# A two-layer network with routed experts: weighting at the eviction, adding gathers, and a regrouped schedule

## The chip, the core and the metric

The kernel runs on one core of a Trainium2 chip. The core has a matrix engine (TensorE, PE in the profile, with PEld for its weight loads), a vector engine (VectorE, DVE), an activation engine (ScalarE, ACT), a general engine (GpSimd, POOL) and an engine that issues most transfers (SyncE, SP). Each works through its own list of instructions in order, and semaphores tie them together. Matrix products land in PSUM, which has eight banks of 128 rows by 512 floats; tiles live in SBUF, 128 partitions wide; tensors of the program and its scratch live in device memory. The metric is the device time of one execution in microseconds (us), less is better. Everything is in 32-bit floats, except the one-hot matrices of the routing, which are in 16 bits. A 32-bit product is issued as two matmul passes, so the profile counts two matmuls for each.

## What is computed

The input has 4 sequences of 1024 tokens with 256 features. Two layers follow each other; each has a sequence part and a feed-forward part, and after each part the input is added and the row normalised:

```python
x = layernorm(x + ssd(x))            # state-space scan, 2 heads of 128, state 64
x = layernorm(x + gelu_mlp(x))       # 256 -> 1024 -> 256
x = layernorm(x + linear_attn(x))    # 16 heads of 16, 64 exponential features, causal
x = layernorm(x + experts(x))        # below

def experts(xf):
    shared = sum(ffn(xf, sw1[i], sw2[i], sw3[i]) for i in range(2))
    rw, sel = top_k(xf @ router_w.T + expert_bias, 2)      # of 8 experts
    rw = softmax(rw)
    combine = einsum("tk,tke->te", rw, one_hot(sel, 8))
    return shared + sum(combine[:, e, None] * ffn(xf, w1[e], w2[e], w3[e]) for e in range(8))

def ffn(x, w1, w2, w3):
    return silu(x @ w1.T) * (x @ w3.T) @ w2.T              # 256 -> 512 -> 256
```

The linear attention keeps, for each head, a running sum of products of key features and values, and a running sum of the key features. An output is the query's features times that sum, divided by the query's features times the sum of keys.

## The kernel before

**Blocks and stream.** The 4096 tokens are 8 blocks of 512, each of 4 tiles of 128 tokens. The stream of a block, `xs[i]`, stays in SBUF from beginning to end and every part adds to it in place.

**Order of the work, first section.** PE's order up to the routed experts is laid out before the program is built: each piece of work is a `Task` with an estimated cost, a rank, the tasks that it comes after with a wait for each, the number of PSUM banks that it takes from one of two pools (6 and 2 banks), and how long it holds them. `trace_tasks` (L239) takes again and again the task that can start first. Only PE is bound to that order; the order of DVE, ACT, POOL and SP is the tool's own, from the dependences and the order in which the program was written. Scan, feed-forward, attention and the first blocks of the shared experts are interleaved in this way.

**Attention.** For a tile of 128 tokens, `scores` makes the masked products of key and query features within the tile, `turn_keys` and `advance` the new contribution to the running sums (`state`), `turn_state` (L667) turns `state` into the stationary tile `kv`, and `outputs` (L627) sums, for each head, the part from the tile itself (`own`, the product with `sc`) and the part from all earlier tiles (the product with `kv`). In `kv` every head has 128 rows, of which 64 hold its state and the others are zero. Four heads fill the four 32-column strips of one bank `ps_o`, and ACT copies the bank to `oraw`.

**Routing.** When the attention of a block is done, `attn_tail` stores its stream turned (`td`) and plain (`xt`) to device memory and `router` (L762) finds the two experts of each token with their weights `wgt`. After the last block `dispatch` (L799) counts the tokens of each expert, gives each token two places (`slot`) in a list that is sorted by expert and padded to 71 tiles, and builds two one-hot matrices for each place: `in_lane` (which row of a tile) and `in_tile` (which tile, times the token's number). `invert` (L882) multiplies them with 64 matmuls into `sent`: which token stands in each row of each tile. All of `dispatch` is traced at one point, in `open_routed`.

**Shared experts.** `shared_jobs` (L890) gives a list of jobs: per block eight hidden jobs (four weight passes for two banks, silu on ACT, the product `gT` on DVE) and four output jobs. Blocks 0 to 4 are run in the first section. Their sums are copied by ACT, stored to device memory (`sd`), and fetched and added again by POOL during the routed stage (`add_part`, L1182). Blocks 5 to 7 are run after the routed experts, and DVE adds their sums straight to the stream (L934).

**Routed experts.** `slot_tiles` (L951) goes over the 71 tiles. `turn` gathers 128 rows of `xt` with an indirect DMA issued by POOL and transposes them, `hidden` multiplies with the weights of the tile's expert (read from a register), `turn_hidden` transposes the result, and `output` multiplies with the second weights, copies (ACT) and stores to `yg`. The gathered tile has six buffers.

**Order of the work, last section.** From the end of the routed stage PE, DVE and ACT run in the order in which the program is written (L1195). After each of the remaining shared jobs one tile is combined (`combine_tile`, L1022): two gathers from `yg`, one for each expert of a token, and two DVE operations that multiply with the weight and add to the stream. When a block lacks nothing, `last_norm` (L1035) computes its statistics and scales on DVE at once, and ACT and SP finish it one job later.

Of the kernel before, what the change touches and what calls it, by code (L numbers as in the profile page):

```python
# [74 lines left out]
def two_layers(ctx: ExitStack, tc: tile.TileContext, x, xT, vecs, cols, wx, w1, w2, wqkv, wout, om, rw, moe, out):  # L75
# [78 lines left out]
    sd = dram.tile([NBLK, P, NT, D], F32, name="sd")  # L154
    xt = dram.tile([NTOK, D], F32, name="xt")
# [4 lines left out]
    wgt = const.tile([P, 2, NTOK // P], F32, name="wgt")  # L160
# [3 lines left out]
    sent = const.tile([P, NSLOT], I32, name="sent")  # L164
    whose = const.tile([1, NSLOT], mybir.dt.int32, name="whose")
# [97 lines left out]
    ssd_end, ffn_end, proj_end, tail_end = {}, {}, {}, {}  # L263
# [208 lines left out]

    def attn_front(hb, wk):
# [109 lines left out]
    def attn_back(hb, wk):  # L583
# [43 lines left out]
        def outputs(j):  # L627

            qf, v1 = front[hb][0], front[hb]["v"]
            tok = slice(j * P, (j + 1) * P)  # L630
            first = hb % 4 == 0 and j == 0
            ps_o = bank(f"ps_o{hb}_{j}", 0)
            for g in range(4):
                for own in ((True,) if first else (False, True)):
                    for c in range(4):
                        h = 4 * g + c
                        f, s = h // 2, h % 2
                        nc.tensor.matmul(  # L638
                            ps_o[c * VW : (c + 1) * VW, g * P : (g + 1) * P],
                            v1[:, j, h, :] if own else kv[:, h, :],  # L640
                            sc[j][f // 4][:, 4 * s + f % 4, :] if own else qf[:, f % 4, f // 4, tok],
                            start=first or not own,
                            stop=own,
                        )
            o[j] = wk.att.tile([P, 4 * P], F32, tag="oraw", name=f"oraw{hb}_{j}", bufs=2)
            nc.scalar.copy(o[j], ps_o)

        def advance(j):
# [3 lines left out]
            for q in range(2):  # L652
                for s in range(2):
                    for r in range(4):
                        nc.tensor.matmul(
                            ps_v[r * VW : (r + 1) * VW, (2 * q + s) * NF : (2 * q + s + 1) * NF],
                            v1[:, j, 8 * q + 2 * r + s, :],
# [9 lines left out]
        def turn_state(j):  # L667
# [4 lines left out]
            for s in range(2):  # L672
                rows = slice(s * NF, (s + 1) * NF)
                nc.scalar.copy(
                    kv[rows].rearrange("p (f s) e -> p f s e", s=2)[:, :, s, :],
                    ps_kv[rows, : 2 * P].rearrange("p (f e) -> p f e", e=VW),
                )
# [517 lines left out]
    with tc.manual_schedule(  # L1195
# [25 lines left out]
        while left:  # L1221
            left.pop(0)()
# [72 lines left out]
```

## Time and profile before

| | before |
|---|---|
| median of 3 runs | 1610.33 us (1609.95 to 1613.02) |
| the profiled execution: its time | 1613.2 us |
| its span, first to last instruction | 1611.5 us |
| PE busy, matmuls | 1518.4 us, 9744 |
| DVE, ACT, POOL busy | 762.5, 605.9, 507.5 us |
| granted PE clock, mean | 0.978 of full |
| gathers of the routed stage, `xe` | 71, 0.944 us of POOL each |
| gathers of the last section, `y` | 64, 0.946 us of POOL each |
| part additions on POOL | 5, 2.35 us each |
| copies of shared sums on ACT, `so` | 10, 0.585 us each |

A line of a timeline gives the start, the length, the engine, the line of the kernel, the operation, output and input tiles, and how many instructions are merged in it; brackets hold the idle time just before it and the instruction that ended it. A line of the list of waits gives who waited, for whom, and then the total, the number of times and the longest. PE's matmuls are pipelined, so the length of one is not the distance between two.

### The profile page before, as it was taken

Reading aid. Unit: us, or ns where it says so; the run is one execution under the profiler, and the core shown is the slowest. Engines: PE = TensorE matmul, PEld = TensorE weight load, DVE = VectorE, ACT = ScalarE, POOL = GpSimd, SP = SyncE. Lnnn points to the kernel's source line nnn. Section 1 sums busy time; section 2 is a strip of 40 time slices with the busy share of each in tenths; the row PEclk is TensorE's granted clock in tenths of the full one; section 3 lists DMA queues with packets and bytes.
Section 4 is the critical chain, followed back from the end, with each engine's and each line's share of the span. In section 5 each row is a group of like instructions: output and inputs, shape, how many; then the busy total and the mean of one; then the engine's idle time right before and its main releaser. Section 6 shows DMA issues by size and latency. Waiting matters only on the chain.

```text
span 1611.5 us, 25591 instructions
## 1 busy us (share of the span) xinstructions
PE 1518.4 (94%) x9744; PEld 998.9 (62%) x9744; DVE 762.5 (47%) x2290; ACT 605.9 (38%) x1065; POOL 507.5 (31%) x524
## 2 busy tenths in 40 slices
PE   8999978999899989899999998999999999999987
PEld 5575656667576757666767665556666666665554
DVE  6977724754646555565544453122222222223765
ACT  2555364454545563554546421122222222221221
POOL 5623323442344332523332215051111111103541
PEclk9999999999999999999999999999999999999999
DMA  8000000000000000200101062331111111111432
GB/s 316 1 1 1 1 1 1 27 1 1 27 2 27 1 14 15 92 27 14 40 1 47 8 231 93 107 112 46 45 44 46 44 46 46 46 33 57 128 101 69
DMA packets 42359, 79.09 MB, mean 49 GB/s; under 512 B 5152, under 2 KB 30880, under 8 KB 40704
## 3 DMA queue, kind: packets, MB, share of 16 engines
q1 hardware_dynamic: 33312, 53.47, 9.3%
q0 software_dynamic: 7200, 20.33, 4.5%
q10 hardware_dynamic: 1728, 3.67, 0.6%
q8 instruction: 80, 1.31, 0.4%
q14 instruction: 39, 0.32, 0.1%
HBM read 52.93 MB, written 24.51 MB: 48 GB/s over the span
## 4 chain that ended last, share of the span: by engine, by line
PE 73%; DVE 14%; ACT 9%; POOL 2%; issue 2%; DMA 0%; SPq 0%; DVEq 0%; ACTq 0%; POOLq 0%
PE ps_ge L975 15%; PE ps_g L908 11%; PE ps_ye L997 8%; PE ps_e L926 6%; PE ps_f L444 5%; PE ps_h L432 5%; PE ps_sc L602 3%; PE ps_o L638 3%; PE ps_gT L990 2%; PE ps_qk L488 2%; PE ps_bc L279 2%; PE ps_k L624 1%; PE ps_p L550 1%; PE ps_v L513 1%; ACT L435 1%
## 5 line engine op out<-in xcount | busy, mean ns | idle before, releaser
L975 PE MATMUL ps_ge<-w,xeT 128*128 x568 | 257.4, 596 | 2.3 <-ACT xeT L968 2.1
L908 PE MATMUL ps_g<-xTs,w 128*128 128x512 f32 x512 | 230.4, 603 | 12.9 <-DVE gT L917 6.8
L958 POOL DMA_INDIRECT xe<-xt,sent x71 | 67.6, 952 | 350.4 <-PE ps_xe L966 329.7
L908 PEld LDWEIGHTS ps_g<-xTs,w 128*128 128x128 f32 x512 | 96.7, 193 | 127.3 <-issue 107.8
L975 PEld LDWEIGHTS ps_ge<-w,xeT 128*128 128x128 f32 x568 | 102.9, 191 | 105.7 <-issue 103.4
L985 DVE TENSOR_TENSOR ge<-se,ps_ge 128x512 f32<-128x512 f32 x71 | 48.8, 687 | 219.1 <-PE ps_ge L975 219.1
L432 PE MATMUL ps_h<-xT,w_sb 128*128 128x512 f32 x256 | 127.8, 643 | 22.3 <-ACT hT L435 12.9
L997 PE MATMUL ps_ye<-w2e,geT 128*128 x568 | 134.4, 379 | 0.0
L926 PE MATMUL ps_e<-w,gT 128*128 128x256 f32 x512 | 120.4, 392 | 10.5 <-DVE x L934 10.5
L444 PE MATMUL ps_f<-w_sb,hT 128*128 128x256 f32 x512 | 118.1, 385 | 1.6 <-ACT hT L435 1.6
L926 PEld LDWEIGHTS ps_e<-w,gT 128*128 128x128 f32 x512 | 99.0, 196 | 30.9 <-DVE x L934 12.9
L997 PEld LDWEIGHTS ps_ye<-w2e,geT 128*128 128x128 f32 x568 | 102.5, 190 | 12.3 <-ACT ye L1005 0.8
L444 PEld LDWEIGHTS ps_f<-w_sb,hT 128*128 128x128 f32 x512 | 96.6, 192 | 17.4 <-issue 3.1
L992 DVE COPY geT<-ps_gT 128x512 f32<-128x512 f32 x71 | 49.1, 692 | 114.4 <-PE ps_gT L990 114.4
L917 DVE TENSOR_TENSOR gT<-sl,ps_g 128x512 f32<-128x512 f32 x64 | 43.9, 686 | 118.0 <-PE ps_g L908 81.8
L432 PEld LDWEIGHTS ps_h<-xT,w_sb 128*128 128x128 f32 x256 | 49.4, 203 | 80.0 <-issue 54.1
L1026 POOL DMA_INDIRECT y<-yg,slot x64 | 63.1, 986 | 99.9 <-PE ps_g L908 47.8
L614 DVE TENSOR_TENSOR sc<-ps_sc,mask_le 128x512 f32<-128x512 f32 x96 | 62.6, 684 | 62.2 <-PE ps_sc L602 53.1
L983 ACT ACTIVATE se<-ps_ge 128x512 f32<-128x512 f32 x71 | 42.4, 597 | 125.5 <-PE ps_ge L975 125.5
L563 POOL TENSOR_SCALAR qf<-qf,csq 128x512 f32<-128x512 f32 x32 | 50.2, 1570 | 116.4 <-ACT qf L561 115.1
L916 ACT ACTIVATE sl<-ps_g 128x512 f32<-128x512 f32 x64 | 37.7, 594 | 130.4 <-PE ps_g L908 100.9
L612 POOL TENSOR_TENSOR sc<-sc,mask_le 128x512 f32<-128x512 f32 x32 | 41.1, 1283 | 133.2 <-ACT sc L611 133.1
(244 smaller groups left out, 2645.6 us busy)
## 6 DMA issues: line engine op xcount, KB each, us to landing
yg<-ye SPq DMA_DIRECT2D x71, 128.0 KB
w<-in_moe SPq DMA_DIRECT2D x8, 1024.0 KB
xt<-in_xT SPq DMA_DIRECT2D x8, 512.0 KB
x<-in_x SPq DMA_DIRECT2D x8, 512.0 KB
xt<-x SPq DMA_DIRECT2D x8, 512.0 KB
td<-xTr SPq DMA_DIRECT2D x16, 256.0 KB
w2e<-in_moe SPq DMA_DIRECT2D x8, 512.0 KB
out<-x SPq DMA_DIRECT2D x7, 512.0 KB
```

Source lines behind the costliest of these rows:

```text
L432: nc.tensor.matmul(ps, w1_sb[:, k, m * P : (m + 1) * P], v.xT[:, k, :], start=(k == 0), stop=(k == KC - 1))
L444: nc.tensor.matmul(v.ps[:, j % 2, :], v.hT[:, m, j * P : (j + 1) * P], w2_sb[:, m, :], start=(m == 0), stop=(m == HID0 // P - 1),)
L563: nc.gpsimd.tensor_scalar_mul(f, f, csq)
L614: nc.vector.tensor_mul(t_s, ps_s, mask)
L908: nc.tensor.matmul(ps[s], w[e][:, 2 * s + k, m * P : (m + 1) * P], xT[i][:, k, :], start=(k == 0), stop=(k == KC - 1),)
L926: nc.tensor.matmul(ps, gT[i, e][:, m, j * P : (j + 1) * P], w2e[:, m, :], start=(e == 0 and m == 0), stop=(e == NSH - 1 and m == HID // P ...
L958: nc.gpsimd.indirect_dma_start(out=xe, out_offset=None, in_=xt, in_offset=bass.IndirectOffsetOnAxis(ap=sent[:, s : s + 1], axis=0),)
L975: nc.tensor.matmul(pg[a], xeT[s][:, k, :], w13[:, bass.ds(e * (4 * HID) + (2 * a + k) * HID, HID)], start=(k == 0), stop=(k == KC - 1),)
L985: nc.vector.tensor_mul(ge[s], se, pg[1])
L992: nc.vector.tensor_copy(geT[s].rearrange("p m t -> p (m t)"), ps)
L997: nc.tensor.matmul(ps[:, :D], geT[s][:, m, :], w2[:, bass.ds(of[s] * (2 * HID) + m * D, D)], start=(m == 0), stop=(m == HID // P - 1),)
L1026: nc.gpsimd.indirect_dma_start(out=y, out_offset=None, in_=yg, in_offset=bass.IndirectOffsetOnAxis(ap=slot[:, n, t : t + 1], axis=0),)
```

## The change

There are six edits.

- **64-row states.** `kv` has one 64-row half for each head, and two heads share a column of it. In `outputs` the product with the past takes 64 rows, from the half that `half_of` gives; heads whose numbers differ by four lie in opposite halves of the array and in different banks, so `ps_o` becomes two banks, with two groups of heads each. The order is: past of two groups, own part of the two, and the same for the other two groups. ACT copies two banks of half a width; `turn_state` copies once. The estimates of the task are changed (1.6 instead of 2.0, two banks, held 1.4).
- **One-hot steps.** `dispatch` returns its eight pairs of comparisons and the list of experts as steps; each is a task of its own among the shared jobs. The token numbers are counted so that the sign of `token_no` says nothing of the place, and the two places of a token are summed in two PSUM areas, which gives `nth`: whether a row of a tile is its token's first or second choice.
- **Direct sums.** The shared sums of blocks 0 to 4 are added by DVE to the stream, two tiles at a time; the copies, stores, loads and additions by POOL are gone. A shared job now comes after the store of its block (`turn_end`).
- **Weights on eviction.** The rows of `xt` have two more columns with the token's two weights, stored by `router`. A gathered tile brings them along; two small DVE operations pick the right one (`xew`), and ACT scales the routed output with it when it evicts it.
- **First tile ahead.** The gather, the transposes and the copy of the first routed tile are a task before the last shared job of the first section.
- **Adding gathers and norms in parts.** `combine` fetches a block's rows with gathers that add into the stream in the DMA itself (`compute_op`), the first choices of four tiles and then the second ones. Five blocks are issued after the second job of the last section, the others after their turn. `last_norm` is cut into sums, scales and finish, each placed behind a job of its own.

```diff
-    xt = dram.tile([NTOK, D], F32, name="xt")
+    xt = dram.tile([NTOK, D + 2], F32, name="xt")
+    xtv = xt.rearrange("(t p) d -> p t d", p=P)
...
+    def half_of(h):
+        return (h ^ h >> 2) & 1
...
-            ps_o = bank(f"ps_o{hb}_{j}", 0)
-            for g in range(4):
+            ps_o = [bank(f"ps_o{hb}_{j}_{n}", 0) for n in range(2)]
+            o[j] = wk.att.tile([P, 4 * P], F32, tag="oraw", name=f"oraw{hb}_{j}", bufs=2)
+            for gs in ((0, 1), (2, 3)):
                 for own in ((True,) if first else (False, True)):
...
+                    for g in gs:
+                        for c in range(4):
+                            h = 4 * g + c
+                            f, s = h // 2, half_of(h)
+                            rows = slice(s * NF, (s + 1) * NF)
+                            nc.tensor.matmul(
+                                ps_o[g % 2][c * VW : (c + 1) * VW, g // 2 * P : (g // 2 + 1) * P],
+                                v1[:, j, h, :] if own else kv[rows, f, :],
+                                sc[j][f // 4][:, 4 * s + f % 4, :] if own else qf[rows, f % 4, f // 4, tok],
...
+            for n in range(2):
+                nc.scalar.copy(
+                    o[j].rearrange("p (g n t) -> p n g t", n=2, t=P)[:, n],
+                    ps_o[n][:, : 2 * P].rearrange("p (g t) -> p g t", t=P),
+                )
...
+            nc.scalar.copy(kv.rearrange("p f e -> p (f e)"), ps_kv[:, : 2 * P])
...
-                lambda j=j: outputs(j), 2.0, r + 0.02, [(t_c, 4.0), (before.get("kv"), 2.5), (far.get("to"), 0.0)], 0, 1, 1.2
+                lambda j=j: outputs(j), 1.6, r + 0.02, [(t_c, 4.0), (before.get("kv"), 2.5), (far.get("to"), 0.0)], 0, 2, 1.4
...
+        nc.sync.dma_start(out=xtv[:, at, D:], in_=wgt[:, at, :])
...
+        def rows(n, t):
...
+        steps = [lambda n=n, t=t: rows(n, t) for n in range(2) for t in range(0, NTOK // P, group)]
+        return steps + [experts], (in_lane, in_tile)
...
+        for n in range(2):
+            for t in range(nt):
+                g = n * nt + t
+                nc.tensor.matmul(ps[:, n, :], in_lane[:, g, :], in_tile[:, g, :], start=(t == 0), stop=(t == nt - 1))
+        no, late = (sm.tile([P, NSLOT], F32, name=n) for n in ("id_no", "id_late"))
+        nc.vector.tensor_copy(late, ps[:, 1, :])
+        nc.vector.tensor_add(no, ps[:, 0, :], late)
+        nc.vector.tensor_single_scalar(nth[:, 1, :], late, 0.0, ALU.not_equal)
+        nc.vector.tensor_scalar(late, no, 0.0, -1.0, ALU.is_gt, ALU.mult)
+        nc.vector.scalar_tensor_tensor(sent, no, float(NTOK // 2), late, ALU.add, ALU.add)
+        nc.vector.tensor_scalar(nth[:, 0, :], nth[:, 1, :], -1.0, 1.0, ALU.mult, ALU.add)
...
-            if not send:
-                nc.vector.tensor_add(xs[i][:, j, :], ps, xs[i][:, j, :])
-            elif j % 2 == 1:
-                so = wk.tile([P, 2, D], F32, tag="so", name=f"so{i}_{j}")
-                nc.scalar.copy(so, at[i])
-                nc.scalar.dma_start(out=sd[i, :, j - 1 : j + 1, :], in_=so)
+            if tiles == 1 or j % 2 == 1:
+                x_j = xs[i][:, j + 1 - tiles : j + 1, :]
+                nc.vector.tensor_add(x_j, at[i][:, j % 2 + 1 - tiles : j % 2 + 1, :], x_j)
...
+    def turn_tokens(s, wx):
+
+        xe = wx.tile([P, D + 2], F32, tag="row", name=f"xe{s}", bufs=6)
+        nc.gpsimd.indirect_dma_start(
+            out=xe,
+            out_offset=None,
+            in_=xt,
+            in_offset=bass.IndirectOffsetOnAxis(ap=sent[:, s : s + 1], axis=0),
+        )
...
+        w = xew[s] = wx.tile([P, 1], F32, tag="xew", name=f"xew{s}", bufs=4)
+        nc.vector.tensor_mul(w, xe[:, D : D + 1], nth[:, 0, s : s + 1])
+        nc.vector.scalar_tensor_tensor(w, xe[:, D + 1 :], nth[:, 1, s : s + 1], w, ALU.mult, ALU.add)
...
-            nc.scalar.copy(ye, ps[:, :D])
+            nc.scalar.activation(ye, ps[:, :D], AF.Identity, scale=xew[s])
...
+    def combine(i):
+
         for n in range(2):
+            for j in range(NT):
+                t = i * NT + j
+                nc.gpsimd.indirect_dma_start(
+                    out=xs[i][:, j, :],
+                    out_offset=None,
+                    in_=yg,
+                    in_offset=bass.IndirectOffsetOnAxis(ap=slot[:, n, t : t + 1], axis=0),
+                    compute_op=ALU.add,
+                )
...
-            after = [(last, wait), (proj_end[2 * i + 1], 10.0)]
+            after = [(last, wait), (turn_end[i], 3.0)]
...
-        Task(close_dispatch, 5.0, 0.0, [(sending, 35.0)], 0, 1)
+        wait = 6.0
+        for _ in range(2 * NTOK // P // 8 + 1):
+            sending = Task(lambda: spaces.steps.pop(0)(), 0.0, 0.0, [(sending, wait)])
+            wait = 3.6
+        sending = Task(close_dispatch, 2.5, 0.0, [(sending, 5.0)], 0, 1)
+
+        turned = Task(lambda: turn_tokens(0, spaces.wx), 0.25, 0.0, [(sending, 8.0), (jobs[-2], 0.0)], 0, 1)
+        jobs[-1].after.append((turned, 0.0))
...
+        fetch = {1: early + amid, 11: late[:1], 12: late[2:], 23: late[1:2]}
+        whole = list(range(NT))
+        norm = {5 + 3 * i: (i, whole) for i in range(NBLK - 2)}
+        norm[28] = NBLK - 2, whole
...
+            for i in fetch.get(n, []):
+                combine(i)
+            if parts:
+                parts.pop(0)()
+            if n in norm:
+                assert not parts
+                parts.extend(last_norm(*norm[n]))
+                parts.pop(0)()
```

## The prediction

> **What bounds the kernel now.** First the totals of the page, then busy time by stretches, then TensorE's (PE's) timeline at the places where a stretch is not full, last the waits of the final stage. PE is the bound, everywhere:
>
> ```profile
> PE 1518.4 (94%) x9744; PEld 998.9 (62%) x9744; DVE 762.5 (47%) x2290; ACT 605.9 (38%) x1065; POOL 507.5 (31%) x524
> ```
>
> So only two things can shorten the run: less PE work, or less of its 93 us of idleness. The routed stage (1062 to 1462 us, 71 slots of 5.82 us) has no idle PE: edits there on other engines are worth nothing while they stay covered. About 50 us are many small gaps in the attention stage (200 to 950 us). The rest sits in three places (PE's timeline: start, length, line, tile, and in brackets the idle time before it with its releaser):
>
> ```profile
> 977.70 11.01 PE L908 MATMUL ps_g<-xTs,w 128*128 128x512 f32 x20 [6.83 <-DVE gT L917]
> ...
> 1046.79 0.44 PE L966 MATMUL ps_xe<-ident,xe 128*128 128x128 f32 x2 [0.68 <-ACT so L937]
> 1049.34 5.40 PE L975 MATMUL ps_ge<-w,xeT 128*128 x8 [2.11 <-ACT xeT L968]
> ...
> 1498.37 7.17 PE L926 MATMUL ps_e<-w,gT 128*128 128x256 f32 x32 [1.47 <-DVE x L934]
> 1506.67 3.72 PE L926 MATMUL ps_e<-w,gT 128*128 128x256 f32 x16 [1.13 <-DVE x L934]
> ...
> 1547.69 9.34 PE L926 MATMUL ps_e<-w,gT 128*128 128x256 f32 x32 [6.38 <-DVE x L934]
> ```
>
> Each gap also slows what follows it: 20 matmul passes take 11.01 us where 8 in a row take 3.43 (so 20 would be 8.6), 32 take 9.34 instead of 7.17, 8 take 5.40 instead of 3.43. The stretches show why (columns: PE, weight load, DVE, ACT, POOL busy, then the granted clock, DMA share, GB/s): the clock falls to a half after the gap.
>
> ```profile
> 971.00:978.00 7.00, 0.30 (x1) 0.30 (x2) 7.00 (x10) 0.86 (x2) 7.00 (x3) 0.80 0.00 0
> 978.00:982.00 4.00, 4.00 (x5) 1.53 (x5) 1.11 (x3) 0.34 (x1) 4.00 (x5) 0.50 0.00 0
> ...
> 1049.00:1052.00 3.00, 2.66 (x5) 1.15 (x6) 0.00 (x0) 0.28 (x1) 1.14 (x2) 0.72 0.50 145
> ...
> 1548.00:1552.00 4.00, 4.00 (x10) 3.19 (x10) 0.51 (x2) 1.41 (x3) 2.02 (x2) 0.50 0.47 155
> ```
>
> **The change, part by part.**
>
> *One-hot steps.* From 960.44 to 974.88 DVE runs the eight pairs of comparisons (0.66 us and 1.14 us start to start, 1.80 a pair) in one burst; two shared products gT, whose silu was ready at 961.2 and 964.6, stand behind it, and PE runs out of banks at 970.9.
>
> ```profile
> 973.67 1.21 DVE L868 TENSOR_TENSOR in_lane<-lane_no,lane 128x1024 f16<-128x1024 f32 x1
> 974.81 1.15 DVE L878 SCALAR_TENSOR_TENSOR own<-tile_no,run,own 1x71 f32<-1x71 f32 x1
> 975.89 0.67 DVE L917 TENSOR_TENSOR gT<-sl,ps_g 128x512 f32<-128x512 f32 x1
> ```
>
> Now they are traced as nine tasks among the shared jobs. A job lasts 3.43 us and a pair plus a gT 1.80 + 0.69 = 2.49, so DVE keeps pace. Gone: 6.83 of waiting and 11.01 - 8.6 = 2.4 of slow clock; I take 9.0 off. POOL's eight products (22.19 us) hide as before. The inversion moves some 5 us later, its matmuls are the same 64, and DVE's six small operations after it delay only the first gather (1001.9 before, read at 1046). The w2e loads behind it on SP's queue move too: 4 MB, first read at 1060. The 0.16 us operations on weights wait for nothing near.
>
> *First routed tile ahead.* Its gather, transposes and copy go before the last shared job, so 0.68 + 2.11 of waiting and 5.40 - 3.43 = 2.0 of slow clock go: 4.8. Against it: the last shared sum is now evicted by DVE (a 128x512 row of DVE takes 0.69) and the first product may need that bank. I take 4.2. The gap of 0.62 in the first slot stays, since no earlier output covers it.
>
> *Direct sums.* Ten ACT copies (0.585 each), ten stores, five loads and five POOL additions (2.35) go; ten DVE additions of 0.69 come, in stages where DVE is about half busy: nothing. They wait for the store of the same rows to xt, long landed: the shared jobs of a block follow it by eight hidden jobs (27 us). The eight weight stores (512 pieces of 8 bytes each) join SP's queue behind each router; what stands behind them, loads for later blocks, has tens of us. If that cover went, 1 to 2 us each.
>
> *Weights on eviction.* ye's copy (0.372 on ACT) becomes a scaled activation; the scaled rows of the last norm take 0.58. ACT is busy 11.4 us in 50 there and ye's bank is wanted 5.8 us later: nothing. The two 128x1 DVE operations per slot (0.16 us each by the norm's small ones) fit in DVE's idle 38 of 50 us, and the gathers they wait for run five slots ahead: nothing.
>
> *64-row states.* Eight passes of four heads take 0.22 us now, four column tiles at once:
>
> ```profile
> 238.37 0.40 PE L638 MATMUL ps_o<-qf,kv 128*32 128x128 f32 x8
> 238.59 0.40 PE L638 MATMUL ps_o<-sc,v 128*32 128x128 f32 x8
> ```
>
> so an output with a past costs 8 x 0.22 = 1.76. Afterwards 16 past passes lie on eight tiles: 0.22 if all overlap. The row for issue is the 32 narrow matmuls of ps_s, 0.58 us, 18 ns each: 16 x 18 = 0.29. The Trainium skill speaks against it twice. "TensorEngine Tiling (Array Packing)", Key Properties, says that changing the tiling mode drains TensorE; the trace prices that: from the last eight ps_o to ps_kv 0.34 instead of 0.22, 0.11 a switch, and each output gets three more (past, own, past, own): 0.33. "TensorE: Matmul & The Clock Gate" (section Wait — 56ns, not 53.3ns?) gives a floor of about 25 ns start to start: then 16 x 25 = 0.40, 2 x 0.40 + 2 x 0.44 + 0.33 = 2.01, 7 us lost over the 28 outputs with a past. The ps_s row undercuts that floor, so I go by the trace: 0.25, between 0.22 and 0.29, gives 1.71, so 1.4 us gained; ends 3 gained, 7 lost. ACT's copy in two (2 x 0.37 for 0.585) and the state's copy in one (0.37 for two of 0.367) cancel.
>
> But PE's order in this stage is laid out from the tasks' estimates, and outputs now claims two banks and 1.6: the whole order shifts, and the 50 us of small gaps with it. No row prices that; taken as nothing, ends 6 gained and 12 lost.
>
> *Indirect adds and norms in parts.* In the last stage DVE runs 64 weighted additions, waits on gathers in its queue, and holds a block's whole norm (4.7 us) ahead of the eviction for which PE waits:
>
> ```profile
> POOL y L1026 <- DVE x L1033: 36.5, 21, 4.1
> ...
> PE ps_e L926 <- DVE x L934: 10.5, 6, 6.4
> ```
>
> Afterwards DVE has products, evictions and norm pieces of 2.1 and 2.6 us. Six 0.52 waits stay in kind (the second output of a bank waits for the eviction of the first): three of them are inside the gaps above, so what goes is 0.95 + 0.61 + 5.86, and 9.34 - 7.17 = 2.2 of slow clock: 9.6. I take 9.0, if the adds keep pace. Now bn_stats waits for the DMAs, and the next gT, so PE, stands behind it. A gather costs POOL 0.946 and 0.30 between (L1026), c = 1.25 an issue, and lands some 2.5 after its start (a DVE wait ended at 1541.93, the gather began at 1539.40). Block i has landed at 1469.8 + (8i+7)c + 2.5; its sums may start at about 1488.2 + 10.4i before PE waits (job 5+3i at 3.43 each, and 3 us that the second pair of banks gives). At 1.25 that leaves 7 us for block 0 and 9 for block 5. It breaks at c = 1.44 (block 5: 1540 against 1472.3 + 47c). The second add to a tile must also wait for the first; four issues, 5 us, lie between, twice the landing.
>
> What an accumulating gather costs, the trace doesn't show. Low: the plain one, 1.25; no reason makes it cheaper. High: the Trainium skill, "Collectives: The Full Stack" (The bandwidth ceiling: the fold count and why AG ≠ RS ≠ AR), says that an adding DMA has two read descriptors per chunk where a copy has one; three for two, if POOL's time follows them, is 1.5 x 0.946 + 0.30 = 1.72 (an estimate), and block 5 would be 13 us late: the sum would be 1609 instead of 1587. The page speaks of another program that makes the descriptors; I take the nearest row, 1.25.
>
> **Sum** against the profiled run (span 1611.5, its time 1613.2): 9.0 + 4.2 + 1.4 + 9.0 = 23.6, so 1589.6. That run stands 0.2% above the median of 1610.33; against the median, 1586.7.
>
> **Rivals.** (1) Everything as above: 1587, chance 0.50, own range 1579 to 1597. (2) The comparisons stay in a burst, since all are ready at 960 and DVE's order is not the hand-written one; for it speaks that the gathers, traced late, already issue at 1001.9. 9 us less: 1596, 0.10. (3) The attention stage loses 10 to 12 by switches or the new order: 1598, 0.17. (4) Adds at c of 1.5 to 1.85: 1603, 0.11. (5) Slower: the adds on POOL at c = 2.0. The last block's gathers land at 1472.3 + 126 = 1598, its norm may wait till 1569: 29 late, and 4 of slow clock: 1587 + 33 = 1620. It decides from c = 1.93. 0.12. Against it: POOL's plain gather is at 0.95 whatever DVE does (0.942 to 1.072).
>
> **How the numbers follow.** The time is that of case 1. The range, 1574 to 1607, leaves out case 5 and the tail of 4, and below it takes in the attention stage's gain. Within 0.2% (1607.1 to 1613.6, about what a measurement here can tell from no change) falls a little of 3 and 4: 0.04; case 5 is slower: 0.12; the rest faster: 0.84.
>
> **What would show it.** No PE gap over 3 us between 950 and 1065; gT between the in_lane rows; no PE wait for an xe copy; PE waits for DVE in the last stage near 3 us, each 0.52; ps_o's groups short, its 28 outputs at 1.7 us. Wrong would be: POOL's DMA_INDIRECT on x well over 1.1 us with bn_stats waiting for DMA, or small gaps before 930 above 60 us in sum.

## The result, and the profile after

The changed kernel is slower, where the prediction said faster.

| | before | after |
|---|---|---|
| median, runs beside each other | 1610.14 us (4 runs, 1609.42 to 1613.02) | 1632.8 us (4 runs, 1631.65 to 1637.4) |
| ratio, 95% interval (the two medians alone give 1.0141) | | 1.0157 (1.0132 to 1.0182) |
| span of the profiled execution | 1611.5 | 1629.9 |
| start to the last router's product `ps_r` | 947.17 | 942.41 |
| `ps_r` to the first routed product `ps_ge` | 102.2 | 95.1 |
| routed stage, to the start of the last `ps_ye` | 415.4 | 413.7 |
| last section, from there to the end | 146.8 | 178.7 |

The stretches are those of one profiled execution each. Three are shorter, by 4.8, 7.1 and 1.7 us; the last one is 31.9 longer. The page's totals of the changed kernel and its group of adding gathers (busy time, mean ns of one, then POOL's idle time before them), and under it the same group of the kernel before:

```profile
PE 1512.1 (93%) x9744; PEld 976.8 (60%) x9744; DVE 759.2 (47%) x2383; ACT 601.6 (37%) x1061; POOL 522.7 (32%) x514
L1051 POOL DMA_INDIRECT x<-yg,slot x64 | 99.2, 1550 | 85.3 <-DMA yg<-ye 46.8
...
L1026 POOL DMA_INDIRECT y<-yg,slot x64 | 63.1, 986 | 99.9 <-PE ps_g L908 47.8
```

In the profiled executions PE is busy for 6 us less and the span is 18 longer: PE waits. And an adding gather takes POOL 1.550 us on the mean where the plain one took 0.986 (median 0.946). PE's timeline of the changed kernel shows where it waits:

```profile
972.07 11.06 PE L950 MATMUL ps_e<-w,gT 128*128 128x256 f32 x50 [1.24 <-DVE gT L941]
982.97 27.63 PE L932 MATMUL ps_g<-xTs,w 128*128 128x512 f32 x64
1010.44 10.52 PE L950 MATMUL ps_e<-w,gT 128*128 128x256 f32 x48
1020.80 2.39 PE L905 MATMUL ps_id<-in_tile,in_lane 128*128 128x71 f16 x64
1030.82 0.69 PE L985 MATMUL ps_xe<-ident,xe 128*128 128x128 f32 x2 [7.64 <-DMA xe<-xt,sent]
1031.30 5.38 PE L950 MATMUL ps_e<-w,gT 128*128 128x256 f32 x16
1037.51 3.67 PE L1002 MATMUL ps_ge<-w,xeT 128*128 x8 [0.83 <-issue]
...
1520.16 11.92 PE L932 MATMUL ps_g<-xTs,w 128*128 128x512 f32 x20 [4.19 <-DVE gT L941]
1538.16 0.70 PE L950 MATMUL ps_e<-w,gT 128*128 128x256 f32 x2 [2.49 <-DVE gT L941]
1574.20 5.37 PE L950 MATMUL ps_e<-w,gT 128*128 128x256 f32 x16 [25.96 <-DVE x L959]
```

The gap of 6.83 at the one-hot steps has become 1.24. DVE's timeline shows why. It still runs the comparisons without a pause, from 955.66 to 976.89, but four products gT now come between them:

```profile
957.46 0.73 DVE L871 TENSOR_TENSOR in_tile<-tile_no,its 128x568 f16<-128x568 f32 x1
958.12 0.67 DVE L941 TENSOR_TENSOR gT<-sl,ps_g 128x512 f32<-128x512 f32 x1
958.72 1.55 DVE L879 TENSOR_TENSOR in_lane<-lane_no,lane 128x1024 f16<-128x1024 f32 x1
...
975.68 1.21 DVE L879 TENSOR_TENSOR in_lane<-lane_no,lane 128x1024 f16<-128x1024 f32 x1
```

But the inversion `ps_id` starts at 1020.80, where in the kernel before it was at 998.91:

```profile
998.91 2.39 PE L887 MATMUL ps_id<-in_tile,in_lane 128*128 128x71 f16 x64
```

So a new gap of 7.64 stands in front of the first gathered tile. And at 1574.20 PE has waited 25.96 us for one eviction. The list of waits in the last section (1440 to 1640 us) names what that eviction stood behind:

```profile
DVE ln_st L1070 <- DMA x<-yg,slot: 49.4, 16, 13.3
PE ps_e L950 <- DVE x L959: 30.1, 6, 26.0
...
POOL x L1051 <- DMA x<-yg,slot: 21.7, 8, 3.5
```

DVE holds a norm's statistics until the adding gathers have landed, and the eviction for PE is behind it in DVE's list. POOL in its turn waits for its own gathers to land. Its timeline:

```profile
1542.88 1.55 POOL L1051 DMA_INDIRECT x<-yg,slot  x1 [0.30 <-issue]
1544.73 1.55 POOL L1051 DMA_INDIRECT x<-yg,slot  x1 [0.30 <-issue]
1548.85 1.55 POOL L1051 DMA_INDIRECT x<-yg,slot  x1 [2.57 <-DMA x<-yg,slot]
1550.70 1.55 POOL L1051 DMA_INDIRECT x<-yg,slot  x1 [0.30 <-issue]
1554.74 1.55 POOL L1051 DMA_INDIRECT x<-yg,slot  x1 [2.49 <-DMA x<-yg,slot]
```

For most of its gathers POOL issues one per 1.855 us (1.55 and 0.30); from 1545 on every second one waits 2.5 to 3.5 us. POOL's order is the tool's own here, and it isn't the written one. A line of the timeline doesn't name its block, but the statistics that each gather releases do: block 7's gathers stand before block 5's, and the last two blocks are issued tile by tile, the second choice right behind the first, so that it must wait until the first has landed (3.8 us after the issue began, by the median of the 64). DVE's timeline shows block 5's four statistics arriving at that rhythm, while PE stands still:

```profile
1552.62 0.43 DVE L1070 BATCH_NORM_STATS2 ln_st<-x 128x6 f32<-128x256 f32 x1 [13.30 <-DMA x<-yg,slot]
...
1558.53 0.43 DVE L1070 BATCH_NORM_STATS2 ln_st<-x 128x6 f32<-128x256 f32 x1 [5.27 <-DMA x<-yg,slot]
...
1570.41 0.43 DVE L1070 BATCH_NORM_STATS2 ln_st<-x 128x6 f32<-128x256 f32 x1 [5.20 <-DMA x<-yg,slot]
...
1570.97 0.39 DVE L959 TENSOR_TENSOR x<-ps_e,x 128x256 f32<-128x256 f32 x1
...
1573.73 0.41 DVE L959 TENSOR_TENSOR x<-ps_e,x 128x256 f32<-128x256 f32 x1
```

The eviction at 1570.97 comes straight behind the last statistics; the next, for which PE waits, stands behind one more part of the norm and ends at 1574.14.

Two stretches of the changed kernel give the price (columns: PE, weight load, DVE, ACT, POOL busy, then granted clock, DMA share, GB/s): 0.80 us of PE work in 25, at a mean clock of 0.51; the 16 passes after the wait take 5.37 us, where 16 elsewhere in this section take 3.62.

```profile
1500.00:1550.00 50.00, 40.59 (x105) 21.39 (x103) 18.45 (x70) 10.06 (x19) 39.87 (x26) 0.90 0.63 111
1550.00:1575.00 25.00, 0.80 (x2) 0.71 (x3) 5.12 (x23) 1.15 (x3) 12.90 (x10) 0.51 0.31 42
```

### The profile page after: what moved, and what is told of

It is laid out like the page before. It is cut to its first block, busy times and chain, and to the rows that moved or that the text cites. A ratio compares the mean times of both kernels' runs of the same rounds, so it can differ in the third digit from the quotient of the medians.

```text
span 1629.9 us, 25587 instructions
## 1 busy us (share of the span) xinstructions
PE 1512.1 (93%) x9744; PEld 976.8 (60%) x9744; DVE 759.2 (47%) x2383; ACT 601.6 (37%) x1061; POOL 522.7 (32%) x514
## 3 DMA queue, kind: packets, MB, share of 16 engines
q0 software_dynamic: 12624, 17.78, 5.8%
## 4 chain that ended last, share of the span: by engine, by line
PE 69%; DVE 12%; ACT 8%; POOL 6%; issue 4%; DMA 1%; SPq 0%; ACTq 0%; DVEq 0%; POOLq 0%
PE ps_ge L1002 15%; PE ps_g L932 8%; PE ps_ye L1024 8%; PE ps_e L950 5%; PE ps_h L433 5%; PE ps_f L445 5%; POOL x L1051 3%; PE ps_sc L608 3%; PE ps_o L647 3%; PE ps_qk L494 2%; PE ps_gT L1017 2%; PE ps_bc L280 2%; PE ps_v L519 1%; PE ps_k L630 1%; PE ps_p L556 1%
## 5 line engine op out<-in xcount | busy, mean ns | idle before, releaser
L433 PE MATMUL ps_h<-xT,w_sb 128*128 128x512 f32 x256 | 123.4, 623 | 21.9 <-ACT hT L436 11.3
L1051 POOL DMA_INDIRECT x<-yg,slot x64 | 99.2, 1550 | 85.3 <-DMA yg<-ye 46.8
L987 ACT COPY xeT<-ps_xe 128x256 f32<-128x256 f32 x71 | 26.7, 376 | 119.4 <-PE ps_xe L985 119.4
```

The source lines that it names most:

```text
L433: nc.tensor.matmul(ps, w1_sb[:, k, m * P : (m + 1) * P], v.xT[:, k, :], start=(k == 0), stop=(k == KC - 1))
L1051: nc.gpsimd.indirect_dma_start(out=xs[i][:, j, :], out_offset=None, in_=yg, in_offset=bass.IndirectOffsetOnAxis(ap=slot[:, n, t : t + 1], ...
```

## The experiments

Theory A says that the loss lies in the last section: the adding gather costs POOL more than a plain one, POOL's order puts them late, and the norms, which come at fixed jobs, hold PE up. The rivals are that the norms' places or the new evictions cost the time whatever the gathers cost, and that the transfers themselves slow the core. A second and separate loss is suspected at the late inversion. In every run the kernel before ran beside the others; its medians were 1611.74 us with the first four kernels below, 1608.08 with the next four, 1607.71 with the last four, and 1610.14 beside the changed kernel, so sums over several sets of runs are good to some 4 us.

**Plain gathers in their place.** The changed kernel without the adding (it leaves out the additions, so the gathered rows overwrite the stream):

```diff
                     in_offset=bass.IndirectOffsetOnAxis(ap=slot[:, n, t : t + 1], axis=0),
-                    compute_op=ALU.add,
                 )
```

> The changed kernel with one thing taken out: the last section's gathers overwrite the stream instead of adding to it (it leaves out the additions; order, waits and number of issues stay). Theory A, the adding gather's price on POOL: 1.85 us an issue falls to about 1.25 (0.95 and 0.30), the first blocks land before their sums are asked for, and the last section, 180 us in the changed kernel's profile, falls to 138 to 146; the total is 1590 to 1600. Theory B, the place of bn_stats in DVE's queue alone, whatever a gather costs: the waits for DMA stay near 49 us and the total stays above 1620. Theory C, contention on the DMA engines: POOL's issue falls but landing and the stretches of DMA share don't, and the total lies between.

Measured: 1598.19 us (1596.88 to 1599.09), ratio 0.9922 (0.9899 to 0.9944). The last section is 144.7 long instead of 178.7, with POOL's order unchanged (it still waits 19.3 us in eight waits). The group of gathers on its page:

```profile
L1051 POOL DMA_INDIRECT x<-yg,slot x64 | 60.5, 945 | 82.9 <-DMA yg<-ye 46.8
```

What is left of the waits in its last section, from the list of waits:

```profile
PE ps_e L950 <- DVE x L959: 9.0, 6, 6.4
DVE ln_st L1069 <- DMA x<-yg,slot: 8.1, 3, 4.1
```

So the adding alone, 0.605 us of POOL each and 1.0 us more until it lands (2.8 against 3.8), makes the section 34 us longer in this order; with plain gathers in the same places the norms and evictions keep pace but for one wait of 6.4. The norms' places alone are not the cause, since the statistics' waits fell from 49.4 us to 8.1.

**Adding gathers early, norms late.** All 64 are issued after the second job, and the norms moved to where they must have landed:

```diff
-        fetch = {1: early + amid, 11: late[:1], 12: late[2:], 23: late[1:2]}
+        fetch = {1: [5, 0, 1, 6, 2, 3, 7, 4]}
         whole = list(range(NT))
-        norm = {5 + 3 * i: (i, whole) for i in range(NBLK - 2)}
-        norm[28] = NBLK - 2, whole
+        norm = {12: (0, whole), 15: (5, whole), 18: (1, whole), 25: (2, whole), 28: (6, whole), 31: (3, whole)}
...
-        for part in last_norm(NBLK - 1, whole[-1:]):
+        for part in last_norm(NBLK - 1, whole[-1:]) + last_norm(4, whole):
             part()
```

> Adding gathers kept at 1.85 us each, but all 64 are issued after the second job in the order of blocks 5, 0, 1, 6, 2, 3, 7, 4, so that each block's adds have landed before its shared sum or its norm is asked for, and the norms stand where their blocks have landed (jobs 12, 15, 18, 25, 28, 31, the last two blocks at the end). Theory A with the wait behind bn_stats: POOL's 64 issues still take 119 us, but PE's 127 us of jobs cover them; PE's waits for DVE in the last section fall from about 33 us to under 6, one more norm lies behind the last job (5 to 8 us), total 1593 to 1603. If the adds hurt in themselves (DMA traffic that slows PE's or DVE's own accesses), PE stays slow and the total stays above 1615.

Measured: 1597.93 us (1595.86 to 1599.35), ratio 0.9921 (0.9897 to 0.9945). Its gathers cost the same 1.549 us each, and in its last section this is what PE waits for:

```profile
PE ps_e L950 <- DVE x L959: 3.1, 6, 0.5
```

Six waits of 0.52, as the prediction had asked for; no statistics wait. The price of the adding is hidden when nothing is due too early, and no slowing of PE by the transfers is seen. The section is still 144.6 long, because the norm of block 4 comes after PE's end.

**The additions on DVE.** Plain gathers into six row buffers, two DVE additions a tile, one tile behind each job from the third on; the norms stay in parts:

```diff
+            y = wk.tile([P, D], F32, tag="row", name=f"y{t}_{n}", bufs=6)
             nc.gpsimd.indirect_dma_start(
-                    out=xs[i][:, j, :],
+                out=y,
...
-                    compute_op=ALU.add,
+            nc.vector.tensor_add(x_j, y, x_j)
...
-        norm = {5 + 3 * i: (i, whole) for i in range(NBLK - 2)}
+        norm = {6 + 4 * i: (i, whole) for i in range(NBLK - 1)}
...
+            if n > 1 and fill:
+                combine_tile(*fill.pop(0), spaces.wx)
```

> The adding gathers alone undone: plain gathers into six buffers, one tile after each job from the third on, and two DVE additions (no weights, these are on the eviction), norms in parts kept and placed one job after a block's last tile. Theory A: POOL 1.25 us an issue, no wait of PE over 3 us in the last section, DVE has 4.7 us of norm, 3.4 of additions and 2.8 of products per four jobs of 13.8 us; the last section is 138 to 142 us, total 1588 to 1596, 14 to 22 us faster than before. If the parts of the norm and the additions still stand in PE's way as before the change, the last section is 147 and the total 1599.

Measured: 1593.45 us (1591.91 to 1594.32), ratio 0.9892 (0.987 to 0.9915). The last section is 139.6 long; PE waits there 5.1 us in six waits, the longest 1.18. DVE has 64 more additions than the changed kernel, of about 0.42 us each, and room for them.

**Steps at every job.** One number: the planner's distance between the one-hot steps.

```diff
-            wait = 3.6
+            wait = 3.4
```

> One number changed: the wait between the one-hot steps is 3.4 instead of 3.6, so that the planner, whose jobs cost 3.5, places a step after every job and not after every second one. Theory: the inversion comes some 30 us earlier, the first gather has landed before PE turns it, the wait of 7.6 us for xe and 1.9 of slow clock go, and everything later shifts: 1621 to 1625 against 1632.8 of the changed kernel. If the late inversion were DVE's or POOL's doing (the products on POOL), PE would wait at the inversion instead and the total stays at 1631 to 1634.

Measured: 1622.38 us (1621.32 to 1630.05), ratio 1.0088 (1.0055 to 1.0121), 10.4 below the changed kernel, with the last section as it was (178.4). PE's timeline of this kernel:

```profile
993.03 2.39 PE L905 MATMUL ps_id<-in_tile,in_lane 128*128 128x71 f16 x64
...
1022.86 0.38 PE L985 MATMUL ps_xe<-ident,xe 128*128 128x128 f32 x2
1023.08 3.62 PE L950 MATMUL ps_e<-w,gT 128*128 128x256 f32 x16
1027.53 3.67 PE L1002 MATMUL ps_ge<-w,xeT 128*128 x8 [0.83 <-issue]
```

A job is planned at 3.5. With 3.6 between steps the plan places a step only after every second job; with 3.4, after every job. The wait of 6.0 before the first step takes two jobs either way, so eight jobs go, at 3.43 us each 27.4. The inversion comes 27.8 us sooner, the 7.64 of waiting for the first gather goes, and the slow passes after it (5.38 us for 16) with it.

The comparisons themselves were not late in the changed kernel. DVE ends its last pair at the same time here as there (975.68 above), since its order isn't the plan's:

```profile
975.44 1.21 DVE L879 TENSOR_TENSOR in_lane<-lane_no,lane 128x1024 f16<-128x1024 f32 x1
```

What the spacing moved is the place of the inversion in PE's order alone.

**Both mends together.** The edits of the last two.

> The changed kernel with both mends: plain gathers with DVE's additions in the last section (as e3_adds_on_dve) and the spacing of 3.4 instead of 3.6 between the one-hot steps (as e4_steps_every_job). If the two losses lie in separate stretches and are independent, the gains add: 1632.8 - 39 - 10.4 = about 1583, ps_ge first at about 1027.5, last section about 137 long, ratio about 0.983. Rival: the earlier start of the routed stage lets the last section meet something new (a transfer, a weight load) and part is given back: 1588 or more.

Measured: 1582.97 us (1582.6 to 1583.6), ratio 0.9841 (0.9817 to 0.9866): the losses were independent, and this version beats both kernels, by 25 us and by 50. PE's last section has six waits, 1.19 and 0.52 us for each block, as at the last one:

```profile
1562.52 7.17 PE L950 MATMUL ps_e<-w,gT 128*128 128x256 f32 x32 [1.19 <-DVE x L959]
1570.21 3.72 PE L950 MATMUL ps_e<-w,gT 128*128 128x256 f32 x16 [0.52 <-DVE x L959]
```

**Adding gathers kept, both orders mended.** The early gathers and late norms (issued after the second job, as the edit above has it), with the spacing of 3.4.

> The adding gathers kept, all 64 issued after the first job with block 5 first and the norms late (as e2_adds_first_norms_late), and the steps spaced by 3.4. If only the order of the adding gathers and the wait of the norms for them cost time, and not the additions in the DMA themselves: about 1587, no PE wait for DVE x over 1 us in the last section. Rival, the adding gathers also slow other work (their traffic, POOL): 1592 or more, some 8 behind e34_both.

Measured: 1589.3 us (1585.66 to 1593.65), ratio 0.9874 (0.9846 to 0.9902), last section 144.6, PE waits for DVE 3.1. The median lies between the two forecasts, 1587 and 1592, and the four runs take in both. It is 6.3 behind the version with additions on DVE: 4.9 of that is the last section, whose end is block 4's norm. The other 1.4 is within the scatter, so a slowing of other work by the adding transfers isn't shown, and isn't needed.

**The attention stage: estimates alone.** The kernel before, with one line of the planner:

```diff
-                lambda j=j: outputs(j), 2.0, r + 0.02, [(t_c, 4.0), (before.get("kv"), 2.5), (far.get("to"), 0.0)], 0, 1, 1.2
+                lambda j=j: outputs(j), 1.6, r + 0.02, [(t_c, 4.0), (before.get("kv"), 2.5), (far.get("to"), 0.0)], 0, 2, 1.4
```

> The kernel before with one edit: the estimates of the outputs task (1.6, two banks, held 1.4, instead of 2.0, one, 1.2), though it still uses one bank and 128-row states. Theory order: the 4.8 us by which the attention stage ended earlier come from the planner's new order, so ps_r ends at 943 to 944 instead of 947.2 and the time falls by 3 to 4.5. Theory shape: they come from the 64-row products and the single copies, and here ps_r stays at 946 to 949 or comes later.

Measured: 1602.72 us (20 runs, 1599.09 to 1607.19) against 1608.08 (33 runs, 1603.89 to 1613.47), ratio 0.9963 (0.9952 to 0.9975): 5.4 us from a line that changes no instruction, only their order. (The two profiled executions differ by 11.3; the one of the kernel before, 1613.2, is at the slow end of its runs.) PE's timeline has the router's product at 943.21, as theory order asks, and after it less of the shared work is left, since two more jobs were placed before it:

```profile
943.21 0.27 PE L772 MATMUL ps_r<-ident,lT 128*128 128x128 f32 x1
...
973.71 3.78 PE L908 MATMUL ps_g<-xTs,w 128*128 128x512 f32 x4 [6.83 <-DVE gT L917]
...
1038.19 5.40 PE L975 MATMUL ps_ge<-w,xeT 128*128 x8 [2.09 <-ACT xeT L968]
```

From `ps_r` to `ps_ge` are 95.0 us, as in the changed kernel, though the burst's gap of 6.83 is still there.

**The 64-row states alone.** The kernel before with the whole edit of the attention (states, two banks, one copy, the estimates), as the diff in the change shows it.

> The kernel before with the whole 64-row edit alone (two banks, past and own in turn, one state copy, the new estimates). Both theories: ps_r at about 942.4 as in the changed kernel, time about 4.8 below before, 1605 to 1606, nothing else moved. The difference from e5_estimates_only is what the shape itself brings. Rival: other parts of the change (the two weight columns, the direct sums, which also lie before that point) brought it, and here ps_r stays near 947.

Measured: 1601.99 us (14 runs, 1599.62 to 1606.42), ratio 0.9964 (0.9952 to 0.9976), `ps_r` at 943.39. Beside the estimates alone that is 0.7 less, within the scatter of both. All of the gain comes from the order; the 64-row shape brings nothing that these runs can tell from zero.

**The burst kept.** The best version with the comparisons traced at one point again:

```diff
-            spaces.steps, spaces.of = dispatch(spaces.wd_pool.__enter__())
+            steps, spaces.of = dispatch(spaces.wd_pool.__enter__())
+            for step in steps:
+                step()
...
-        wait = 6.0
-        for _ in range(2 * NTOK // P // 8 + 1):
-            sending = Task(lambda: spaces.steps.pop(0)(), 0.0, 0.0, [(sending, wait)])
-            wait = 3.4
-        sending = Task(close_dispatch, 2.5, 0.0, [(sending, 5.0)], 0, 1)
+        sending = Task(close_dispatch, 2.5, 0.0, [(sending, 35.0)], 0, 1)
```

> e34_both with the one-hot edit undone: the comparisons are traced at one point again, in a burst, and the inversion is placed 35 after it as in the kernel before; all else kept. If the step-by-step tracing is what removed the gap at 972: a PE wait of about 6.8 for gT comes back with 2 of slow clock after it, less the 1.24 that was left: 7 to 8 slower than e34_both, 1590 to 1591. Rival: with the new order of the tasks the burst meets spare banks and costs nothing: 1583 to 1585.

Measured: 1590.89 us (1590.19 to 1596.12), 7.9 above the best version. PE's timeline has the old gap, to the hundredth, where the steps had left 1.24:

```profile
972.83 3.78 PE L932 MATMUL ps_g<-xTs,w 128*128 128x512 f32 x4 [6.83 <-DVE gT L941]
```

**The first tile late.** The best version with the first routed tile turned after the last shared job:

```diff
-        turned = Task(lambda: turn_tokens(0, spaces.wx), 0.25, 0.0, [(sending, 8.0), (jobs[-2], 0.0)], 0, 1)
-        jobs[-1].after.append((turned, 0.0))
...
+        turn_tokens(0, wx)
         for s in range(NSLOT):
             hidden(s)
```

> e34_both with the first routed tile fetched and turned after the last shared job again, as in the kernel before. If moving it ahead is worth what the gaps showed: waits of 0.7 and 2.1 and about 1.7 of slow clock come back, 0.83 of waiting for a bank goes: 3.5 to 4 slower, 1586.5 to 1587. Rival: the eviction of the last shared sum or the bank takes the gain: within 1 of e34_both.

Measured: 1585.07 us (1584.66 to 1589.81), 2.1 above the best version, between the two theories. PE's timeline:

```profile
1028.30 0.41 PE L985 MATMUL ps_xe<-ident,xe 128*128 128x128 f32 x2 [0.83 <-issue]
1029.69 3.67 PE L1002 MATMUL ps_ge<-w,xeT 128*128 x8 [0.98 <-ACT xeT L987]
```

The waits are 0.83 and 0.98 now, where the kernel before had 0.68 and 2.11, and no slow clock follows (3.67 instead of 5.40). So there was less left to gain. In the kernel before, ACT's copy of the tile had waited for the store of the last shared sum to land:

```profile
1048.91 0.37 ACT L968 COPY xeT<-ps_xe 128x256 f32<-128x256 f32 x1 [2.18 <-DMA sd<-so]
```

That store is gone with the direct sums, and the copied tile lies in another pool now; which of the two freed the copy wasn't run.

**Adding gathers of 64 rows.** What the price follows: each gather of the previous kernel with adding gathers, cut in half.

```diff
+                for h in (slice(0, P // 2),):
...
-                    out=xs[i][:, j, :],
+                        out=xs[i][h, j, :],
...
-                    in_offset=bass.IndirectOffsetOnAxis(ap=slot[:, n, t : t + 1], axis=0),
+                        in_offset=bass.IndirectOffsetOnAxis(ap=slot[h, n, t : t + 1], axis=0),
```

> e24_adds_early_steps with each adding gather cut to the first 64 of its 128 rows; leaves out the additions of the other 64 rows of each tile. If POOL's price follows the rows (about 0.012 a row for an adding gather, 0.007 for a plain one): 0.78 instead of 1.549 us each. Rival, a fixed price of an adding gather on top of that of a plain one (1.549 - 0.945 = 0.60): 0.47 + 0.60 = 1.07. A plain gather's own fixed part would bring both values up by some tenths.

Measured, from the page:

```profile
L1052 POOL DMA_INDIRECT x<-yg,slot x64 | 91.0, 1422 | 66.0 <-DMA yg<-ye 46.8
```

Both expectations were wrong. Half the rows save 0.128 of 1.550 us, 2 ns a row; if that holds down to few rows, about 1.29 us are fixed for each instruction (an estimate from these two points). How a plain gather's 0.945 divides wasn't run.

**The written order on POOL.** The changed kernel with POOL, too, held to the order of the program in the last section:

```diff
-        engines={mybir.EngineType.PE, mybir.EngineType.DVE, mybir.EngineType.Activation}
+        engines={mybir.EngineType.PE, mybir.EngineType.DVE, mybir.EngineType.Activation, mybir.EngineType.Pool}
```

> The changed kernel with one edit: POOL too runs the last section in the order in which the program is written, so block 5's eight adding gathers come right after block 4's and block 7's after them, first choices of four tiles ahead of the second ones. Theory price and order: the price of 1.855 an issue alone makes block 5 land at 1455.7 + 48 x 1.855 + 3.8 = 1548.5, 9 after its norm is due at 1539, and block 6 at 1578, 4 to 6 late; so of the 25.7 of waiting for block 5 5 to 9 stay and a few are added at block 6: 1605 to 1614, POOL waits near 0. Theory order alone (at 1.855 the adds would still be in time): about 1600, as e2_adds_first_norms_late. Theory price alone (the tool's order costs nothing): still above 1625.

Measured: 1607.45 us (20 runs, 1603.76 to 1610.63), ratio 0.9994 (0.9983 to 1.0005): 25 us of the loss were POOL's order. Price and order both count, and their shares overlap (plain gathers in the tool's order had taken 34 off the section): the gathers are still too slow for the norms, statistics wait 27.3 us in 20 waits, and the last section is 153.5 long, 6.7 more than in the kernel before. PE's timeline has several small waits where the changed kernel had one of 25.96, some of them for norms ahead of block 5's:

```profile
1521.88 10.55 PE L932 MATMUL ps_g<-xTs,w 128*128 128x512 f32 x20 [3.64 <-DVE gT L941]
1538.01 0.70 PE L950 MATMUL ps_e<-w,gT 128*128 128x256 f32 x2 [2.99 <-DVE gT L941]
1541.42 1.22 PE L950 MATMUL ps_e<-w,gT 128*128 128x256 f32 x2 [2.71 <-DVE gT L941]
...
1554.33 3.72 PE L950 MATMUL ps_e<-w,gT 128*128 128x256 f32 x16 [2.01 <-DVE x L959]
```

## Why the prediction was wrong

**Indirect adds and norms in parts (9.0 off): wrong, about 41 us.** The section became 31.9 longer. Two steps failed.

- *"I take the nearest row, 1.25."* Measured 1.855 (1.55 and 0.30), above the upper end of 1.72 that was worked out from the read descriptors of an adding DMA: 1.550 to 0.945 is a ratio of 1.64, not 1.5, and the half gathers show that most of the price is per instruction, so scaling it by descriptors had the wrong form as well. (The sum given for 1.72, 1609, is 22 above 1587, of which the working shows only block 5's 13.) The landing is 3.8, not 2.5. The break-even, 1.44, was worked out rightly; the value under it was taken from a plain gather because that was the nearest row, though the one argument about the adding itself pointed to 1.72.
- *"Block i has landed at 1469.8 + (8i+7)c + 2.5"* and *"four issues, 5 us, lie between"* assume the written order on POOL. The description of the kernel says that only PE, DVE and ACT are bound there. The tool put block 7 before 5, eight issues of 1.855 late, and paired the adds of a tile, so that the second waits for the first. Restoring the order gives 25 us back. With it the formula does well for the time: a forecast of 1605 to 1614 with c = 1.855 stood before that run, and it took 1607.45, though earlier norms than block 5's waited too. Why the tool chose its order isn't known.

Rival 5 had the right mechanism, adds on POOL too slow and the norm behind them, but placed it at c = 2.0 and at the last block, and gave it 0.12. By its own numbers the last block is late from c = 1.53 on (1569 - 1472.3, over 63 issues); the 1.93 from which it "decides" has no working. It came at 1.855, at block 5, through the order.

**One-hot steps (9.0): right in size, its next step wrong.** The gap went from 6.83 to 1.24, the slow clock with it, and undoing the edit costs 7.9. The comparisons did stay back to back on DVE, as rival 2 had it, but with the products between them, and that was enough. But *"The inversion moves some 5 us later … delay only the first gather (1001.9 before, read at 1046)"* failed: it moved 22 us later, because 3.6 between the steps is more than the 3.5 at which a job is planned, and the read moved ahead of the last job at the same time. That cost 10.4, more than the edit gained. A planner's wait has to be compared with its grid before it is called small.

**First routed tile ahead (4.2): 2.1 measured.** The bank wait was foreseen, and is 0.83. What was over-counted is the slow clock and half of the wait: in the best version with the tile late again they don't come back, so other edits of the same change had already taken them.

**64-row states (1.4 by the shape, 0 by the order): right in sign, wrong in source.** Past and own passes with their switches take 1.79 us an output after the change (two pairs from 234.55 to 236.34), 1.76 before and 1.71 in the prediction. The first lines of the second pair:

```profile
235.50 0.45 PE L647 MATMUL ps_o<-qf,kv 64*32 64x128 f32 x16
235.88 0.65 PE L647 MATMUL ps_o<-sc,v 128*32 128x128 f32 x16
```

Sixteen past passes and the switch behind them take 0.38 where sixteen took 0.44 before, but the own passes that a switch follows take 0.57 (from 234.93 to 235.50) where the last ones, with none behind, take 0.46: 0.11 for a switch. The Trainium skill's page "TensorEngine Tiling (Array Packing)" (Key Properties) says that changing the mode drains TensorE; this trace shows the 0.11, and the switches take what the overlap gives. The re-ordering, *"taken as nothing, ends 6 gained and 12 lost"*, brings 5.4, near its gaining end. Where those come from is only partly shown: up to the first routed product PE idles 72.8 us with the new estimates and 74.4 before, but is busy 965.4 instead of 974.9 with the same work, so most of the difference between these two traces is time at a lower clock. How much of that a run catches varies (the version with both mends and the one that keeps the adding gathers, with the same order of this stage, had `ps_r` at 943.28 and 948.35), so the single traces can't say which gap the new order spares; the medians can say that it does.

**Direct sums, weights on eviction (nothing): right for the routed stage.** PE doesn't wait there, and no wait of PE for weight columns or `xew` is seen. The 1.7 us by which the stage is shorter are its first eight passes, 3.67 instead of 5.40. The direct sums may have a share in the first tile's gain, as said.

The sum, in medians: the predicted 1586.7; POOL's order 25.4; the price of the adds against norms that come too early 9.5 (written order against adds early and norms late); the late inversion 10.4; 1.1 and 2.1 too much at the steps and the first tile; 4.0 too little in attention. That makes 1631.2. To it belong 6.8 more, by which the section with adds early and norms late is itself longer than the forecast (144.6 against 137.8, its end being block 4's norm). So the terms give 1638.0 where 1632.8 was measured, and from sets of runs whose kernel before differed by 4 us no closer sum can be asked. For the last section alone, within the traces, they do add up: 25.2, 8.9 and 6.8 are the 40.9 by which it missed.

## What to carry to other kernels

An operation that the trace doesn't show should not be given its nearest row's price when the plan breaks 15% above that row: the forecast is then about that price, and belongs on the side where the one argument about the new operation points. Work that is moved to an engine whose order is not written out needs that engine's real order, not the program's, before any landing time is computed from it. And in a plan with a grid of jobs, a distance just above the grid costs a whole job each time: here eight jobs, and 10.4 us of the run.

## What the runs showed that was not expected

- An adding gather of 128 rows of 1 KB costs POOL 1.549 us and lands 3.8 us after its start; a plain one 0.945 and 2.8. With 64 rows it still costs 1.421 and lands after 3.1.
- The packets of POOL's queue rise with it: 12624 against 6480 (in the version with additions on DVE) for the same 17.78 MB. The 6480 are 48 for each of 135 plain gathers; with the same for the 71 unchanged ones, that is 144 for an adding gather and 48 for a plain one.
- Sixteen 64-row products and a switch take 0.38 us (235.50 to 235.88), so such narrow passes start less than 24 ns apart, switch included; still nothing was gained that the runs can tell from zero, since each output has more switches.
- A different order of the same instructions in the attention stage moved the median by 5.4 us, where the new shape of the products moved it by 0.7.
